# When VectorE's queue reaches its work: conversions and tables moved in the prologue of a graph-attention kernel

## Chip, cores and metric

One core of one Trainium2 chip. The metric is device time in microseconds of one execution. Engines: TensorE (PE in the profile), VectorE (DVE), ScalarE (ACT), GpSimd (POOL) and SyncE (SP), each with its own queue, worked through in order. DMAs are issued from the queues of SP, ACT and POOL.

## What is computed

One layer of a graph network on 12500 nodes of 256 features and 200000 edges sorted by their destination:

```python
h = relu(layernorm(x))                         # x: 12500 x 256
q, k, v = h @ Wq + bq, h @ Wk + bk, h @ Wv + bv     # 8 heads of 32
logits = sum(q[dst] * k[src], over 32) / sqrt(32)   # 200000 edges x 8 heads
attn = softmax of the logits over the edges of one dst
agg = segment_sum(attn * v[src], dst)
o = gelu(agg + h @ Wskip + bskip)
x = x + layernorm(h + o) * gamma + beta
```

## The kernel before

It works in two stages. **The prologue** (`project`, L156, and `make_plan`, L422) makes tables in DRAM. **The walk** (`walk_streams`, L760) goes along the edges, gathers rows of those tables and reduces them. The walk begins when the prologue has ended: its first instructions stand behind a branch (L349) on a flag that the plan computes.

`project` goes over 98 blocks of 128 nodes, in 23 groups of 1, 2, 4, then sixteen times 5, then 4, 4, 2 and 1 blocks (L168). `prepare(g)` (L201) loads the x tile of group g+2 (L180, three buffers), takes mean and variance of each block (L211, L215), their factors (L221, L222), and ACT makes h (L226). For each block PE transposes h (L140) and ACT copies that to SBUF (L142); PE then multiplies it with the weights of keys and values (L257, into ps_kv, three buffers) and of queries (L263, into ps_q, one buffer). VectorE evicts both, adding the bias: L260 for keys and values, L267 for queries. ACT and POOL split q into two parts (L268, L269), and SP stores h, kv and q (L272, L274).

Among this stands other work of VectorE, put there by a scheduler that places each instruction by its own estimate of when its inputs are there; "kept order" dependencies (`behind`, L161) hold an instruction back behind another one of its engine without a semaphore:

- `pieces` (L112, called in group 3): the biases as three bf16 parts.
- `make_near` (L703, called in group 4): the tables of node offsets, near and near_n, 48 partitions wide, in five parts. Each part has two iotas of POOL (L711, tiles near_m and near_g, one buffer each, so the iota of a part waits for L753 of the part before) and some ten operations of VectorE (L740 to L753). Its first operation (L716) is kept behind the factors of the latest group. The walk reads these tables (L1052, L1063).
- `make_plan`: loads the destinations (L406, L408), checks their order (L443 to L446), writes them and the sources to DRAM (L441, L449), computes where each of 8 streams starts (L459 to L478), and gathers the chunks of all streams, 66 x 8 x 384 destinations and as many sources, with 16 indirect DMAs of POOL (L488). VectorE casts them to float: L507 the destinations (df), L492 the sources (sf). From df come the first node of each step (L512 to L517, stored and read back by L518, L519 as one row, d0_row), what L523 to L608 make of that row, the masks and offsets of L636 to L683 that go to e_tab and pen_tab, and at last the flag (L700). sf is transposed by PE (L496, kept behind the products of blocks from the middle on) and cast into idx (L504), by which the walk gathers.

The lines that set the gathers and casts:

```python
488   nc.gpsimd.indirect_dma_start(out=t[:, s, :CH], ..., ap=at_i[:, s:s + 1]...)
492   nc.vector.tensor_copy(sf[:, :, :CH], sch)
507   nc.vector.tensor_copy(df[:, :, :CH], dch[:, :, :CH])
```

Of the kernel before, what the change touches and what calls it, by code (L numbers as in the profile page):

```python
# [34 lines left out]
OP = mybir.AluOpType  # L35
# [12 lines left out]
S = 8  # L48
K = 3
CH = K * P  # L50
# [20 lines left out]
def gnn_kernel(ctx: ExitStack, tc: tile.TileContext, x, src, dst, Wq, bq, Wk, bk, Wv, bv,  # L71
               Wskip, bskip, gamma, beta, out):
    nc = tc.nc
    N, HID = x.shape
# [4 lines left out]
    KV = 2 * HID  # L79
# [25 lines left out]
    def weights(t, w):  # L105
        return nc.sync.dma_start(t, w.rearrange("(c p) n -> p c n", p=P))

    def rows(t, a):
        return nc.scalar.dma_start(t, bass.AP(tensor=a.tensor, offset=a.offset,
                                              ap=[[0, t.shape[0]], [1, HID]]))  # L110
# [26 lines left out]
    def transposed(pool, psum, h):  # L137
        ps = psum.tile([P, KC, P], F32, name="ps_t")
        for c in range(KC):
            nc.tensor.transpose(ps[:, c, :], h[:, c * P:(c + 1) * P], ident)  # L140
        hT = pool.tile([P, KC, P], F32, name="hT")
        return hT, nc.scalar.copy(hT, ps)  # L142
# [13 lines left out]
    def project():  # L156


        last, turned, products = None, None, []

        def behind(ins, other):  # L161
            tc.add_manual_dep(ins.ins, other.ins.name, mybir.DependencyInfo(
                mybir.DependencyClass.NoSync, mybir.DependencyReason.DATA), reason="kept order")

        sizes = [1] * NBLK
        if NBLK >= 14:
            mid = NBLK - 14
            sizes = [1, 2, 4] + [5] * (mid // 5) + [mid % 5] * (mid % 5 > 0) + [4, 2, 1]  # L168
        with tc.tile_pool(name="proj_c", bufs=1) as cpool, \
# [21 lines left out]
            b_q = cpool.tile([P, HID], F32, name="b_q")  # L191
# [41 lines left out]
            for g, (b0, n) in enumerate(zip(starts, sizes)):  # L233

                if g > 1 and g + 1 < len(sizes):
                    ready[g + 1] = prepare(g + 1)
                if g == 4:
                    make_near(tc, near, near_n, lambda ins: behind(ins, last))
                if g == 3:
                    for ins in [rows(gam, gamma)] + \  # L240
                            [weights(w_s, Wskip)]:
                        behind(ins, products[-1])
                    pieces(b_s3, bskip, 1.0)
                    pieces(b_o3, beta, 1.0)
                    zero = cpool.tile([WN, HID], F32, name="zero")
                    nc.vector.memset(zero, 0.0)
                    for k in range(2):
                        behind(nc.scalar.dma_start(q_pc[NP:, k * HID:(k + 1) * HID], zero),
                               products[-1])
                h = ready.pop(g)  # L250
                kvo = pool.tile([P, 5, KV], F32, name="kvo")[:, :n, :]
                qp = pool.tile([P, 5, 2, HID], F32R, name="qp")[:, :n]
                for b in range(n):
                    hT, turned = transposed(pool, psum, h[:, b, :])
                    ps_kv = psum.tile([P, 2 * HID], F32, name="ps_kv", bufs=3)
                    for c in range(KC):
                        ins = nc.tensor.matmul(ps_kv, hT[:, c, :], w_kv[:, c, :], start=c == 0,  # L257
                                               stop=c == KC - 1)
                    products.append(ins)
                    nc.vector.tensor_tensor(kvo[:, b, :], ps_kv, b_kv, op=OP.add)  # L260
                    ps_q = psum.tile([P, HID], F32, name="ps_q", bufs=1)
                    for c in range(KC):
                        ins = nc.tensor.matmul(ps_q, hT[:, c, :], w_q[:, c, :], start=c == 0,  # L263
                                               stop=c == KC - 1)
                    products.append(ins)
                    q = qp[:, b, 1, :].bitcast(F32)
                    nc.vector.tensor_tensor(q, ps_q, b_q, op=OP.add)  # L267
                    nc.scalar.copy(qp[:, b, 0, :], q)  # L268
                    nc.gpsimd.tensor_tensor(qp[:, b, 1, :], q, qp[:, b, 0, :].bitcast(F32),  # L269
                                            op=OP.subtract)  # L270
                for tab, t in ((h_tab, h), (kv_tab, kvo)):
                    nc.sync.dma_start(tab[b0 * P:(b0 + n) * P, :]  # L272
                                      .rearrange("(p b) d -> p b d", p=P), t)
                nc.sync.dma_start(q_pc[b0 * P:(b0 + n) * P, :]  # L274
                                  .rearrange("(p b) d -> p (b d)", p=P),
                                  qp.rearrange("p b k d -> p (b k d)").bitcast(F32))
                if g < 2:
                    ready[g + 1] = prepare(g + 1)
        return products

    def queries(q_tab):

# [41 lines left out]
    NST = -(-(LEN + LEN // 128) // (CH - 1))  # L324
# [10 lines left out]
    idx = pl.tile([P, S, K, NST], I32, name="idx")  # L335
    d0_row = pl.tile([1, NST * S], I32, name="d0_row")
    slot_row = pl.tile([1, NSLOT // 2, 4], I32, name="slot_row")
    near = pl.tile([6 * S, QT * P], BF16, name="near")
    near_n = pl.tile([6 * S, 4 * WNN + 4 * WN], BF16, name="near_n")
    e_tab = dram.tile([NST, 6 * S, CH], BF16, name="e_tab")  # L340
    pen_tab = dram.tile([NST, 2, S, CH + 1], F32, name="pen_tab")
    with tc.tile_pool(name="pln", bufs=1) as pool, tc.tile_pool(name="pln_e", bufs=1) as ep, \
            tc.tile_pool(name="pln_ps", bufs=1, space=PSUM) as psum:
        products = project()
        make_plan(tc, pool, ep, psum, src, dst, N, LEN, NST, SLACK, NT, dram, ident, flag,
                  idx, d0_row, slot_row, e_tab, pen_tab, products, 4 * HID, 4 * KV)
    fits = nc.values_load(flag[0:1, 0:1], min_val=0, max_val=1)
    many = nc.values_load(flag[0:1, 2:3], min_val=0, max_val=1)
    with tc.If(fits > 0) as branch:  # L349
# [47 lines left out]

def load_edges(nc, pool, a, E, C, fill, name):

    t = pool.tile([P, C], I32, name=name)  # L400
    full, rest = divmod(E, C)
    nc.vector.memset(t, fill)

    for lo, hi in ((0, full // 16 * 16), (full // 16 * 16, full)):
        if lo < hi:
            nc.gpsimd.dma_start(t[lo:hi], a[lo * C:hi * C].rearrange("(p c) -> p c", c=C))  # L406
    if rest:
        nc.gpsimd.dma_start(t[full:full + 1, :rest], a[full * C:].rearrange("(p c) -> p c", p=1))  # L408
    return t


def load_next(nc, pool, dst, E, C, N):

    nxt = pool.tile([P, 1], I32, name="nxt_i")
    nc.vector.memset(nxt, N)
    starts = E // C if E % C else E // C - 1
    nc.gpsimd.dma_start(nxt[:starts], bass.AP(tensor=dst.tensor, offset=dst.offset + C,
                                              ap=[[C, starts], [1, 1]]))
    return nxt


def make_plan(tc, pool, ep, psum, src, dst, N, LEN, NST, SLACK, NT, dram, ident, flag, idx, d0_row,  # L422
              slot_row, e_tab, pen_tab, products, bytes_x, bytes_row):

    nc = tc.nc
    E = src.shape[0]
    STEP = CH - 1
    C = -(-max(E, (S - 1) * LEN + SLACK + STEP * NST + 1) // P)  # L430
    dst_p = dram.tile([1 + P * C, 1], I32, name="dst_p")
    src_p = dram.tile([1 + P * C, 1], I32, name="src_p")
    d0_d = dram.tile([NST, S], I32, name="d0_d")
# [26 lines left out]
    last = pool.tile([NST, S], F32, name="last")  # L460
# [23 lines left out]
    dch = pool.tile([NST, S, CH + 1], I32, name="dch")  # L484
    sch = pool.tile([NST, S, CH], I32, name="sch", tag="sch")
# [3 lines left out]
                out=t[:, s, :CH], out_offset=None, in_=tab[:, :],  # L489
                in_offset=bass.IndirectOffsetOnAxis(ap=at_i[:, s:s + 1], axis=0))  # L490
    sf = pool.tile([NST, S, CH + 1], F32, name="sf")
    nc.vector.tensor_copy(sf[:, :, :CH], sch)  # L492
    for s in range(S):
        ps = psum.tile([P, K, NST], F32, name="ps_i")
        for j in range(K):
            ins = nc.tensor.transpose(ps[:, j, :], sf[:, s, j * P:(j + 1) * P],  # L496
                                      ident[:NST, :NST])
# [6 lines left out]
        nc.vector.tensor_copy(idx[:, s], ps)  # L504

    df = pool.tile([NST, S, CH + 1], F32, name="df")
    nc.vector.tensor_copy(df[:, :, :CH], dch[:, :, :CH])  # L507

    nc.vector.tensor_copy(df[0:1, 1:, 0:1], df[0:1, 1:, 1:2])
    nc.vector.memset(df[0:1, 0:1, 0:1], 0.0)  # L510
# [9 lines left out]
                                      ap=[[0, 1], [1, NST * S]]))  # L520

    line = pool.tile([1, 2, S], F32, name="line")
    nc.vector.tensor_copy(line[:, 0, :], d0_row[:, :S])  # L523
    nc.vector.tensor_copy(line[:, 1, :], d0_row[:, (NST - 1) * S:])
    nn = pool.tile([1, S + 1], F32, name="nn")
    nc.vector.memset(nn, float(N))
    nc.vector.tensor_copy(nn[:, :S], line[:, 0, :])
# [11 lines left out]
    F = NST * S  # L539

    done = ep.tile([1, 2, F], F32, name="done2", tag="chk_d")
    done, more_b = done[:, 0], done[:, 1]
# [6 lines left out]
    nc.vector.tensor_scalar(lead_i, lead_i, P - 1, None, op0=OP.bitwise_and)  # L549
    nc.vector.tensor_copy(lead, lead_i)  # L550
    nc.vector.tensor_scalar(lead, lead, -1.0, float(P - 1), op0=OP.mult, op1=OP.add)
    nc.vector.tensor_copy(done[:, :F - S], d0_row[:, S:])
    nc.vector.tensor_tensor(done3[:, :NST - 1], done3[:, :NST - 1],
                            nn[:, None, :S].to_broadcast([1, NST - 1, S]), op=OP.subtract)
    nc.vector.tensor_copy(done3[:, NST - 1], cnt[:, 0])
# [58 lines left out]
    for i, size in enumerate((bytes_x, bytes_row)):  # L614
        nc.vector.tensor_scalar(slot_row[:, :, 2 * i:2 * i + 2],
                                ps[:, i, :M].rearrange("o (m b) -> o m b", b=2), float(size),
                                None, op0=OP.mult)
# [46 lines left out]
    def row(r, make):  # L664
# [5 lines left out]
                                             op=OP.is_equal))  # L670
# [1123 lines left out]
```

## Time and profile before

| | us |
|---|---|
| median of three runs (2444.04 to 2455.95) | 2448.26 |
| the profiled execution, its own time | 2449.12 |
| its span, first to last instruction | 2447.3 |
| prologue: last eviction of block 97 (L267) ends | 355.6 |
| walk: first gather (L1035) starts | 359.1 |

The profiled execution is 0.9 us above the median. Busy shares of the span are PE 70%, DVE 82%, ACT 44% and POOL 68%; as averages over two stages of different kind they say little on the prologue, which has to be read from its own stretch.

How to read the lines shown below. A line of the timeline has the start and the duration in us, the engine, the line of the program, the operation, output and inputs with partitions x elements and type, how many instructions are merged, and in brackets how long the engine sat idle before it and what ended that. A line of the waits has who waited for whom, the total in us, how many times, and the longest. A line of the table of stretches has the stretch, its length, the busy time of each engine with its count of instructions, the granted TensorE clock (1.00 is full speed), the busy share of the 16 DMA engines and what they moved.

### The profile page before, as it was taken

Reading aid. Unit: us, or ns where it says so; the run is one execution under the profiler, and the core shown is the slowest. Engines: PE = TensorE matmul, PEld = TensorE weight load, DVE = VectorE, ACT = ScalarE, POOL = GpSimd, SP = SyncE. Lnnn points to the kernel's source line nnn. Section 1 sums busy time; section 2 is a strip of 40 time slices with the busy share of each in tenths; the row PEclk is TensorE's granted clock in tenths of the full one; section 3 lists DMA queues with packets and bytes.
Section 4 is the critical chain, followed back from the end, with each engine's and each line's share of the span. In section 5 each row is a group of like instructions: output and inputs, shape, how many; then the busy total and the mean of one; then the engine's idle time right before and its main releaser. Section 6 shows DMA issues by size and latency. Waiting matters only on the chain.

```text
span 2447.3 us, 29473 instructions
## 1 busy us (share of the span) xinstructions
PE 1708.7 (70%) x7824; PEld 909.6 (37%) x7824; DVE 1999.8 (82%) x2461; ACT 1066.4 (44%) x2328; POOL 1658.1 (68%) x1745
## 2 busy tenths in 40 slices
PE   6879983555557767767777767676676777677765
PEld 3445542222223333333333334333333343343333
DVE  7866856777778898898888888888888988888884
ACT  3333321333334544554545444445444444445443
POOL 4342447777777777777777777777777777777740
PEclk9999995666667777776667676677677767767678
DMA  7656668888888988888888988899889888889862
GB/s 259 253 207 264 251 250 263 256 255 254 255 268 266 286 276 282 285 277 284 279 285 279 287 271 282 274 285 288 275 282 287 282 281 284 277 279 287 279 202 76
DMA packets 306128, 649.33 MB, mean 265 GB/s; under 512 B 52836, under 2 KB 192238, under 8 KB 300954
## 3 DMA queue, kind: packets, MB, share of 16 engines
q0 software_dynamic: 128768, 423.23, 55.7%
q1 hardware_dynamic: 176434, 223.46, 27.2%
q8 instruction: 64, 1.05, 0.2%
q10 hardware_dynamic: 748, 0.66, 0.1%
q14 instruction: 114, 0.93, 0.1%
HBM read 538.91 MB, written 108.23 MB: 264 GB/s over the span
## 4 chain that ended last, share of the span: by engine, by line
DMA 25%; PE 23%; DVE 19%; issue 12%; POOL 10%; ACT 8%; SPq 3%; DVEq 0%; another core or an unknown queue 0%; ACTq 0%; POOLq 0%
DMA kv<-kv_tab,idx 16%; POOL kv L1035 9%; PE ps_kv L257 5%; DVE kv L1084 5%; DMA h<-h_tab 4%; PE ps_a L867 4%; DVE vw L1139 3%; DVE L L1091 3%; PE ps_qe L1075 3%; PE ps_q L263 3%; PE ps_a L1165 2%; ACT L987 2%; PE ps_hot L909 2%; DMA out_dram<-o 2%; SPq L837 2%
## 5 line engine op out<-in xcount | busy, mean ns | idle before, releaser
L1035 POOL DMA_INDIRECT kv<-kv_tab,idx x1576 | 1521.3, 965 | 482.4 <-issue 342.6
L1084 DVE TENSOR_TENSOR kv<-ps_qe,kv 128x1024 f32<-128x1024 f32 x394 | 468.8, 1218 | 191.1 <-DMA kv<-kv_tab,idx 117.9
L1139 DVE TENSOR_TENSOR vw<-ps_x,kv 128x2048 f32<-128x2048 f32 x197 | 449.4, 2281 | 9.1 <-PE ps_x L1126 9.1
L1091 DVE TENSOR_REDUCE L<-kv 128x64 f32<-128x2048 f32 x197 | 450.4, 2286 | 6.9 <-DMA et<-e_tab 0.2
L1075 PE MATMUL ps_qe<-qw,to_e 64*128 64x256 f32 (+1 forms) x1576 | 312.6, 396 | 107.5 <-DVE kv L1084 102.6
L1054 ACT ACTIVATE to_e<-ps_hot,ones 128x384 fp32r<-128x384 f32 x396 | 210.4, 573 | 316.1 <-PE ps_hot L1052 308.0
L1075 PEld LDWEIGHTS ps_qe<-qw,to_e 64*128 64x128 f32 (+1 forms) x1576 | 223.8, 248 | 272.7 <-DVE kv L1084 168.4
L1165 PE MATMUL ps_a<-vw,to_n 128*32 128x264 f32 (+1 forms) x2344 | 280.3, 516 | 4.2 <-DVE vw L1146 3.7
L1177 ACT COPY sums_w<-ps_a 128x264 f32<-128x264 f32 x130 | 49.2, 378 | 498.3 <-PE ps_a L1165 439.7
L1099 PE MATMUL ps_x<-ident,L 128*64 128x128 f32 x197 | 73.1, 371 | 274.0 <-DVE vw L1146 205.2
L1052 PE MATMUL ps_hot<-et,near 48*128 48x384 bf16 x396 | 142.5, 420 | 136.5 <-ACT to_e L1054 131.8
L257 PE MATMUL ps_kv<-w_kv,hT 128*128 128x512 f32 x392 | 194.8, 619 | 15.3 <-ACT hT L142 14.2
L269 POOL TENSOR_TENSOR qp<-qp 128x256 fp32r<-128x256 f32 x98 | 88.4, 903 | 171.8 <-ACT qp L268 171.6
L867 PE MATMUL ps_a<-w_s,hT 128*128 128x256 f32 x368 | 171.9, 648 | 21.2 <-ACT hT L853 18.0
L1165 PEld LDWEIGHTS ps_a<-vw,to_n 128*32 128x32 f32 (+1 forms) x2344 | 99.3, 139 | 216.2 <-issue 174.4
L1099 PEld LDWEIGHTS ps_x<-ident,L 128*64 128x64 f32 x197 | 25.7, 130 | 362.7 <-DVE vw L1146 288.3
L1165 PE MATMUL ps_hot<-vw,to_n 128*64 128x264 f32 x808 | 144.8, 509 | 1.9 <-DVE o L915 1.1
L1183 ACT COPY kv<-ps_a 1x264 f32<-1x264 f32 x388 | 142.9, 368 | 6.3
L867 PEld LDWEIGHTS ps_a<-w_s,hT 128*128 128x128 f32 x368 | 115.6, 329 | 69.0 <-ACT hT L853 44.1
L987 ACT ACT_TABLE_LOAD x102 | 130.9, 1283 | 1.7
L1065 ACT ACTIVATE to_n<-ps_hot,ones 128x384 f32<-128x384 f32 x197 | 103.6, 578 | 53.7 <-PE ps_hot L1063 51.8
L263 PE MATMUL ps_q<-w_q,hT 128*128 128x256 f32 x392 | 106.1, 395 | 24.3 <-DVE qp L267 24.2
(278 smaller groups left out, 2103.2 us busy)
## 6 DMA issues: line engine op xcount, KB each, us to landing
qw<-q_pc SPq DMA_DIRECT2D x264, 128.0 KB
kv<-kv_tab,idx POOLq DMA_INDIRECT x1576
kv_tab<-kvo SPq DMA_DIRECT2D x16, 1280.0 KB
q_pc<-qp SPq DMA_DIRECT2D x16, 1280.0 KB
qw<-q_pc SPq DMA_DIRECT2D x264, 64.0 KB
table<-sums_w SPq DMA_DIRECT2D x264, 61.9 KB
pen<-pen_tab SPq DMA_DIRECT2D x66, 192.5 KB
sums<-table SPq DMA_DIRECT2D x92, 132.0 KB
```

The costliest lines, as they stand in the source:

```text
L257: ins = nc.tensor.matmul(ps_kv, hT[:, c, :], w_kv[:, c, :], start=c == 0, stop=c == KC - 1)
L263: ins = nc.tensor.matmul(ps_q, hT[:, c, :], w_q[:, c, :], start=c == 0, stop=c == KC - 1)
L867: self.keep(nc.tensor.matmul(self.ps[:, b, :], self.hT[:, b, c, :], w_s[:, c, :], start=False, stop=False, skip_group_check=True))
L987: keep(nc.scalar.activation(dummy[:, 1:2], dummy[:, 0:1], function))
L1035: ins = keep(nc.gpsimd.indirect_dma_start(out=t[:, s, :], out_offset=None, in_=kv_tab[:, :], in_offset=bass.IndirectOffsetOnAxis(ap=idx[:, ...
L1054: keep(nc.scalar.activation(step[c]["to_e"][:, i, :], ps[:, :CH], AF.Relu, scale=-1.0, bias=ones))
L1075: keep(nc.tensor.matmul(ps[:, b, a, :], g["to_e"][at:at + w, i, j * P:(j + 1) * P], g["qw"][at:at + w, i, :], start=True, stop=True))
L1084: keep(nc.vector.tensor_tensor(k, g["qe", half].rearrange("p b a d -> p a b d"), k, op=OP.mult))
L1091: keep(nc.vector.tensor_reduce(g["L"][:, j, :].rearrange("p (s h) -> p s h", s=S), g["kv"][j][:, :, :HID].rearrange("p s (h d) -> p s h d" ...
L1139: keep(nc.vector.tensor_tensor(t[:, :, HEADS:].rearrange("p s (h d) -> p s h d", h=HEADS), wj[:, :, :, None].to_broadcast([P, S, HEADS, D] ...
L1165: keep(nc.tensor.matmul(ps[at:at + w, :], g["to_n"][:, j, i * P + at:i * P + at + w], g["vw"][j][:, s, :], start=j == 0, stop=j == tiles_o ...
L1183: keep(nc.scalar.copy(step[c + 1]["kv"][0][0:1, s, HID - HEADS:], ps[at:at + 1, :]))
```

## The change

`project` now returns its evictions of the queries (L267) in order as well, as `biased`. `make_plan` keeps five casts behind one of them, counted in hundredths of the 98 blocks: the destinations (L507) behind block 35 (36 hundredths), the sources (L492) behind block 42 (43), and three casts of d0_row (L523, L524, L552) behind block 44 (45). With 16 groups or more, `make_near` is called in group 13 (whose first block is 57) where it was called in group 4 (block 12), and `pieces`, with the loads of gamma and Wskip and the two stores of zeros, in group 12 where it was group 3. Nothing is computed differently, and no instruction is added or left out. Lines from 431 on move by seven.

```diff
-                if g == 4:
+                if g == (4 if len(sizes) < 16 else 13):
                     make_near(tc, near, near_n, lambda ins: behind(ins, last))
-                if g == 3:
+                if g == (3 if len(sizes) < 16 else 12):
                     for ins in [rows(gam, gamma)] + \
                             [weights(w_s, Wskip)]:
                         behind(ins, products[-1])
...
-                    nc.vector.tensor_tensor(q, ps_q, b_q, op=OP.add)
+                    biased.append(nc.vector.tensor_tensor(q, ps_q, b_q, op=OP.add))
...
+    def behind(ins, share):
+
+        tc.add_manual_dep(ins.ins, biased[len(biased) * share // 100].ins.name,
+                          mybir.DependencyInfo(mybir.DependencyClass.NoSync,
+                                               mybir.DependencyReason.DATA), reason="kept order")
...
-    nc.vector.tensor_copy(sf[:, :, :CH], sch)
+    behind(nc.vector.tensor_copy(sf[:, :, :CH], sch), 43)
...
-    nc.vector.tensor_copy(df[:, :, :CH], dch[:, :, :CH])
+    behind(nc.vector.tensor_copy(df[:, :, :CH], dch[:, :, :CH]), 36)
...
-    nc.vector.tensor_copy(line[:, 0, :], d0_row[:, :S])
-    nc.vector.tensor_copy(line[:, 1, :], d0_row[:, (NST - 1) * S:])
+    behind(nc.vector.tensor_copy(line[:, 0, :], d0_row[:, :S]), 45)
+    behind(nc.vector.tensor_copy(line[:, 1, :], d0_row[:, (NST - 1) * S:]), 45)
...
-    nc.vector.tensor_copy(done[:, :F - S], d0_row[:, S:])
+    behind(nc.vector.tensor_copy(done[:, :F - S], d0_row[:, S:]), 45)
```

## The prediction

> **What bounds the kernel now.** The chain of work that ended last, taken over the first 600 us, shows two stages. Until 355 us it runs through PE's projection matmuls (L257 19.8% of that stretch, L263 10.8%); after that through the gathers of the walk (POOL L1035, DMA kv) and VectorE's L1084, L1091 and L1139. The change touches the first stage alone, so I read that one: 98 blocks, each with two transposes, a key/value product (L257) and a query product (L263), both evicted by VectorE (L260, L267).
>
> PE's timeline gives its pace and where it loses it. Columns: start, duration, instruction, and in brackets the idle time before it with what ended it.
>
> ```profile
> 78.78 1.60 PE L263 MATMUL ps_q<-w_q,hT 128*128 128x256 f32 x4 [2.64 <-DVE qp L267]
> 80.17 3.15 PE L257 MATMUL ps_kv<-w_kv,hT 128*128 128x512 f32 x4
> ...
> 134.31 2.07 PE L263 MATMUL ps_q<-w_q,hT 128*128 128x256 f32 x4 [4.05 <-DVE qp L267]
> ...
> 154.61 2.07 PE L263 MATMUL ps_q<-w_q,hT 128*128 128x256 f32 x4 [6.56 <-DVE qp L267]
> ...
> 208.72 1.98 PE L257 MATMUL ps_kv<-w_kv,hT 128*128 128x512 f32 x4
> ...
> 214.88 1.98 PE L257 MATMUL ps_kv<-w_kv,hT 128*128 128x512 f32 x4
> ```
>
> From 208.72 to 214.88 PE does two blocks: **3.08 us a block** when nothing holds it. The three upper stalls have one cause: ps_q has a single buffer, so the query product of a block waits until VectorE has evicted that of the block before. I count the starts of L257 block by block: block 0 at 12.58, 7 at 46.99, 17 at 86.64, 28 at 120.14, 41 at 177.22, 57 at 227.20, 97 at 352.23. Against 3.08 a block, the stretch 7-17 is 8.9 us late (39.65 for 30.8), 17-28 on time (33.5 for 33.9), 28-41 **17.0 late** (57.08 for 40.04), 41-57 0.7 and 57-97 1.8 late. The first seven blocks lose 12.9 to loads and first transposes.
>
> Who holds VectorE is in its waits of the first 480 us (total, times, longest) and in its own timeline:
>
> ```profile
> DVE kvo L260 <- PE ps_kv L257: 42.7, 35, 2.3
> ...
> DVE st L211 <- DMA x_in<-in_x_dram: 10.0, 6, 4.3
> ...
> DVE sf L492 <- DMA sch<-src_p,at_i: 7.9, 1, 7.9
> DVE df L507 <- DMA sch<-src_p,at_i: 6.0, 1, 6.0
> DVE near_s L740 <- POOL near_m L711: 5.0, 4, 2.1
> ```
>
> ```profile
> 131.39 1.94 DVE L507 CAST df<-dch 66x3072 f32<-66x3072 int32 x1 [5.96 <-DMA sch<-src_p,at_i]
> ...
> 151.22 1.76 DVE L492 CAST sf<-sch 66x3072 f32<-66x3072 int32 x1 [7.94 <-DMA sch<-src_p,at_i]
> ```
>
> The first line of the waits is harmless: VectorE waiting for PE means PE is the bound. The casts L507 and L492 are the fault: VectorE's queue is in order, each stands in it before its gathered chunk has landed, and the evictions behind it wait too. PE's 4.05 and 6.56 us of idle follow from them.
>
> The table of stretches says the same in busy time (PE, PEld, DVE, ACT, POOL, then granted clock, DMA share, GB/s):
>
> ```profile
> 47.00:87.00 40.00, 32.84 (x101) 17.83 (x102) 33.79 (x107) 11.58 (x31) 15.26 (x21) 0.96 0.48 177
> 87.00:120.00 33.00, 31.51 (x108) 18.46 (x107) 26.67 (x83) 15.47 (x40) 13.82 (x19) 1.00 0.95 335
> 120.00:177.00 57.00, 42.37 (x134) 24.23 (x132) 39.29 (x108) 14.96 (x39) 26.88 (x30) 0.91 0.58 218
> 177.00:258.00 81.00, 78.31 (x287) 47.40 (x287) 48.14 (x139) 33.85 (x89) 22.05 (x28) 1.00 0.70 257
> ```
>
> In 177-258 VectorE is busy 48 of 81 us and PE 78: there is room for VectorE's work. In 47-87 it is busy 33.8 of 40, beside waits: the near tables stand there.
>
> **The change part by part.** How VectorE's queue stands in the built program, counted in evicted blocks (L260) ahead of an instruction, before and after: sorted check (L445) 19 and 9; offsets for the gathers (L478) 25 and 15; L507 29 and 37; the big subtraction L640 31 and 39; L492 33 and 52; the node-row conversions L523 and L552 35 and 53; L573 40 and 60; the near tables 6 to 15, and, but for part 0's first six operations, 41 to 51. L492 is pinned only behind block 42; the scheduler puts it after the near tables. The last of the plan (L700) stands at 89 and 90.
>
> *The two waits.* The gathers issue from 113.97 to 142.14 on POOL, the first chunk has landed by 131.39 and the second by 151.22: 17 and 37 us after the first issue. After the change they start some ten blocks earlier, at block 15, and the casts stand 22 and 37 blocks later (68 and 114 us at 3.08). Both waits go, and with them the whole loss of 28-41: two stalls, the slowed matmuls behind each (2.07 for 1.03) and the 4.27 us wait for an x tile before, which gathers, x loads and the src store shared the queues with. **-17.0**. If only the two waits go and the x wait stays, it is 1.8 less (PE's idle of 1.82 at 123.83).
>
> *The node row.* Its way from L517 (135.4) to L523 (156.38) took 21 us, POOL's gathers in between; after, 39 to 53 is 14 blocks, 43 us. 0. L573 to L589 (way through DRAM) had 8.0 us (175.9 to 183.9), with 0.74 of wait left; after it has again three blocks, 9.2 us. Between 0 and +1; I take 0. The transposes of sf (L496) stand on PE behind block 52's products, L492 on VectorE ahead of that block's eviction; as ps_q keeps PE close behind VectorE, I take 0, at most +1.8 (L492's own time).
>
> *The near tables, gone from 6-15.* Their groups sum to 25.9 us of durations (four parts of 256 columns 19.5, the one of 128 4.2, small ones 2.2); starts lie some 0.07 closer than durations over 72 operations, so 21, and 5.0 of waits for POOL's iota. In their place the plan's first checks move up: L402 1.0, L445 2.0, L446 1.7, L459 0.7, L463 1.2, L466 1.2 and small ones 1.6, 9.4, with 1.7 of part 0. A block's own work on VectorE is 1.40 (L260 0.61, L267 0.34, L211 0.34, L215 and the factors 0.11, start to start), so each block leaves 1.68: over blocks 7-17 16.8, more than 11.1. PE should keep pace: up to **-8.9**. Against it stand the x loads. Groups now come due sooner in a stretch where DMA share was 0.80 (12-47); landings took 5.3 and 6.5 us (issue 101.97, 114.94; use 107.30, 121.45), with three buffers. Cost from 0 to the whole 8.9; I give +3, two waits of the size that cost PE 1.82 less a little overlap. Net **-5.9**.
>
> *The near tables, now in 41-51.* About 19 us of work fall on ten blocks with 16.8 free, then L492 1.7 and the first idx casts. Each part's L740 waits for an iota that starts only when L753 of the part before is done (1.5 us, behind which one or two evictions fit): four waits that were 5.0 in all. Below: VectorE's backlog is worked off in 52-63 without PE stopping, 0. Above: 2.2 + 1.7 + 5.0 = 8.9. As ps_q is single, I go near the middle, **+4.5**. 57-97 is the same work in the same order but for the k chain (some 5 us later on blocks that had room): 0, bounds -1 and +3. POOL moves the iotas of four parts (near_m of 1.5 or 1.2 us each, near_g 0.4); its subtractions have 2 to 4 us of idle each, so only the store of q lags. The loads of gamma, W_s and the zero rows (0.4 MB) go to block 52 or so on ACT's and SP's queues: at 257 GB/s there, 0.
>
> Here the TensorE clock is weighed. After 2.64 us of idle the next eight matmuls took 1.60 + 3.15 instead of 1.03 + 1.88: 1.84 lost. The Trainium skill (TensorE: Matmul & The Clock Gate, What's actually happening) puts the fall to half clock at an idle window of about 3.4 us. By it, stalls of 1 to 2 us in the middle cost no clock, and the sum stays; by the row one long one might add 1.8.
>
> **The sum:** -17.0 - 5.9 + 4.5 = -18.4. The walk starts when block 97 is done (its first gather comes 4 us after), and keeps its length. The profiled execution, 2449.1 us (span 2447.3 and 1.8 around it), lies 0.9 over the median of three (2448.3). 2449.1 - 18.4 = 2430.7; against the median 2429.9. I say **2430**.
>
> **Rivals.** *The x loads take the early gain* (0.14): 87-120 ran at 0.95 of DMA, and the same bytes now come sooner. Nothing in 7-17, two or three landings waited for later at 1.82 each: -17.0 + 4.5 + 4.5 = -8, 2441; range 2437 to 2444. Against: 47-87 used 0.48. *VectorE becomes the bound in 41-57* (0.11): 8.9 with one cold clock 1.8, and 2 more in 57-63: -17.0 - 5.9 + 12.7 = -10, 2439, range 2436 to 2446. *All of it pays* (0.08): early stretch on pace, middle nearly free: -17.0 - 8.9 + 1 = -25, 2424 and down to 2418. *Slower* (0.06): one mechanism, x tiles late at VectorE's L211. If six groups between blocks 7 and 41 each wait a whole landing of 6.5 us, that is 39 against 25.9 given up, with 4.5 in the middle: +17.6, 2467. It decides from four groups on (21.4 / 6.5 = 3.3). *The pins move nothing* is ruled out by the queue order. The forecast keeps 0.61, 2424 to 2437.
>
> Range 2420 to 2442: it leaves out the slow ends of the first two rivals, the slower case and the lowest of the best one, some 0.2. About 0.5%, 12 us, is what a measurement of this kernel can tell from no change, so faster means under 2436: the forecast but for its upper edge and the best case, 0.68; same 0.26, slower 0.06.
>
> **What the next profile would show.** No wait of L492 or L507 (now L499, L514) for DMA; no idle of PE over 3 us behind L267 after block 7; L257 of block 41 near 154 instead of 177; iota waits of about 1 us each now between 155 and 185 us with short PE stalls behind L267 there; the first walk gather near 340 instead of 359. Wrong if: x_in waits over 10 us in the first 120; PE falling behind more than 9 us in 41-57; or a walk longer than 2088 us (359 to the end) by more than 3.

## The result

| | before | after |
|---|---|---|
| median (6 runs each) | 2448.48 (2444.04 to 2455.95) | 2432.33 (2431.09 to 2434.58) |
| ratio, 95% interval | | 0.9935 (0.9922 to 0.9948) |
| profiled execution, own time | 2449.12 | 2432.86 |
| last eviction (L267) of block 97 starts | 355.2 | 334.8 |
| first gather of the walk | 359.1 | 339.1 |
| first gather to the end of the span | 2088.2 | 2092.0 |

The kernel is 16.1 us faster, 0.65%; the forecast was 2430. The prologue gained 20.05 us where 18.4 were forecast, and the walk of the profiled pair gave 3.8 back. In the first eight experiments the walk alone took 2633 to 2713 us, so their totals are compared only with runs of the kernel before made beside them; their prologues kept the same pace.

PE's timeline of after (columns as before) has four stalls of more than 0.3 us behind L267 left after block 7, and none over 2.70 us:

```profile
161.55 1.13 PE L263 MATMUL ps_q<-w_q,hT 128*128 128x256 f32 x4 [0.55 <-DVE qp L267]
...
175.43 1.13 PE L263 MATMUL ps_q<-w_q,hT 128*128 128x256 f32 x4 [0.86 <-DVE qp L267]
...
179.77 1.13 PE L263 MATMUL ps_q<-w_q,hT 128*128 128x256 f32 x4 [0.49 <-DVE qp L267]
...
185.32 1.13 PE L263 MATMUL ps_q<-w_q,hT 128*128 128x256 f32 x4 [2.70 <-DVE qp L267]
```

All four lie where the tables now stand. Seen from the block that waits, each is VectorE being late; the records before them show why. VectorE's waits of the first 480 us in after:

```profile
DVE kvo L260 <- PE ps_kv L257: 44.2, 29, 2.3
...
DVE st L211 <- DMA x_in<-in_x_dram: 11.1, 9, 3.6
```

No cast waits for a DMA any more (13.9 us before), and the x tiles cost VectorE 1.1 more than before. The rise lies ahead of block 7: between 48 and 180 us the waits for x tiles fell from 6.2 to 3.8 us, the longest from 4.3 to 1.2. The stretches of after (PE, PEld, DVE, ACT, POOL, clock, DMA share, GB/s):

```profile
47.00:87.00 40.00, 37.96 (x130) 22.03 (x129) 32.36 (x103) 14.63 (x39) 25.66 (x30) 1.00 0.91 343
87.00:120.00 33.00, 31.21 (x110) 18.35 (x109) 16.90 (x46) 13.26 (x36) 12.92 (x17) 1.00 0.72 258
120.00:177.00 57.00, 53.06 (x180) 30.49 (x178) 42.34 (x120) 22.25 (x57) 22.80 (x29) 1.00 0.72 263
177.00:258.00 81.00, 75.19 (x269) 43.78 (x270) 74.99 (x206) 31.27 (x80) 30.04 (x31) 1.00 0.65 248
```

In 47-87 PE is busy 37.96 of 40 us instead of 32.84, in 120-177 53.06 instead of 42.37. In 177-258 it lost 3 us of busy time, and VectorE rose from 48 to 75 us of 81.

For all kernels below I read one thing: the starts of VectorE's eviction of the queries (L267, 98 records in every profile). "Late" is the time of a stretch less 3.08 us a block. The order within a pair of blocks shifts a start by up to 1.5 us, so only differences of one column count.

| kernel | block 7 at | late 7-17 | 17-41 | 41-57 | 57-97 | block 97 at | first gather | ratio to before, 95% |
|---|---|---|---|---|---|---|---|---|
| before | 52.0 | 7.0 | 16.5 | 1.5 | 1.1 | 355.2 | 359.1 | |
| after | 48.7 | 0.5 | -0.8 | 7.5 | 1.6 | 334.8 | 339.1 | 0.9935 (0.9922-0.9948) |
| after_again | 48.8 | 0.9 | -0.9 | 7.8 | 1.6 | 335.4 | 339.6 | 0.9948 (0.9932-0.9965) |
| pins_only | 51.8 | 5.5 | 2.0 | 1.5 | 1.3 | 339.2 | 343.1 | 0.9986 (0.9964-1.0008) |
| tables_only | 48.9 | 2.8 | 11.8 | 7.8 | 1.5 | 349.9 | 353.9 | 0.9991 (0.9971-1.0011) |
| near8 | 48.3 | 1.7 | 10.2 | 1.5 | 1.5 | 340.5 | 344.5 | 0.9928 (0.9905-0.9951) |
| near9 | 46.7 | 3.1 | 10.2 | 2.6 | 1.0 | 340.8 | 344.8 | 0.9935 (0.9915-0.9956) |
| near17 | 49.4 | 0.5 | -0.7 | 1.5 | 7.8 | 335.7 | 339.6 | 0.9964 (0.9945-0.9983) |
| spread7_p3 | 50.7 | 3.0 | 5.3 | 1.6 | 1.3 | 339.1 | 343.1 | 0.9957 (0.9940-0.9973) |
| spread13_p3 | 50.5 | 4.7 | -0.8 | 4.9 | 3.7 | 340.2 | 344.4 | 0.9956 (0.9939-0.9972) |
| thin | 49.8 | 3.3 | 0.0 | 8.0 | -0.4 | 337.9 | 342.1 | 0.9928 (0.9915-0.9942) |
| thick | 50.2 | 1.7 | 5.4 | 1.6 | 1.6 | 337.7 | 341.6 | 0.9928 (0.9915-0.9942) |
| no_tables | 48.9 | 1.9 | -0.9 | 1.8 | 1.4 | 330.3 | 334.2 | 0.9910 (0.9897-0.9924) |
| thin_k | 47.4 | 2.3 | -0.1 | 2.8 | 0.2 | 329.9 | 334.1 | 0.9925 (0.9911-0.9939) |

Each row is one profile. The two of the changed kernel agree within 0.6 us at every column but the ratio, but thin and thin_k, whose programs are alike in these blocks, are 2.4 us apart at block 7, so single rows scatter by that much there. The ratios scatter more: a few us of the prologue are hardly seen in them.

### The profile page after: what moved, and what is told of

Its sections match the earlier page's. It is cut to its first block, busy times and chain, and to the rows that moved or that the text cites. A ratio compares the mean times of both kernels' runs of the same rounds, so it can differ in the third digit from the quotient of the medians.

```text
span 2431.1 us, 29470 instructions
## 1 busy us (share of the span) xinstructions
PE 1704.8 (70%) x7824; PEld 904.9 (37%) x7824; DVE 2000.1 (82%) x2461; ACT 1067.8 (44%) x2328; POOL 1671.5 (69%) x1745
## 4 chain that ended last, share of the span: by engine, by line
DMA 26%; PE 21%; DVE 17%; POOL 13%; issue 13%; ACT 6%; SPq 2%; POOLq 0%; DVEq 0%; another core or an unknown queue 0%; ACTq 0%
DMA kv<-kv_tab,idx 19%; POOL kv L1042 13%; PE ps_kv L257 5%; DVE kv L1091 4%; DVE vw L1146 4%; DVE L L1098 4%; DMA h<-h_tab 3%; PE ps_a L874 3%; PE ps_q L263 3%; PE ps_qe L1082 2%; PE ps_a L1172 2%; ACT L994 1%; SPq L844 1%; DMA out_dram<-o 1%; PE ps_hot L1059 1%
## 5 line engine op out<-in xcount | busy, mean ns | idle before, releaser
L257 PE MATMUL ps_kv<-w_kv,hT 128*128 128x512 f32 x392 | 193.7, 615 | 16.1 <-ACT hT L142 15.3
L269 POOL TENSOR_TENSOR qp<-qp 128x256 fp32r<-128x256 f32 x98 | 97.4, 994 | 155.2 <-ACT qp L268 154.9
```

## The experiments

**The two halves.** pins_only keeps the pins and calls tables and pieces in groups 4 and 3; tables_only has the tables late and no pins. In pins_only

```diff
-                if g == (4 if len(sizes) < 16 else 13):
+                if g == (4 if len(sizes) < 16 else 4):
-                if g == (3 if len(sizes) < 16 else 12):
+                if g == (3 if len(sizes) < 16 else 3):
```

and in tables_only, for this and the other four casts,

```diff
-    behind(nc.vector.tensor_copy(sf[:, :, :CH], sch), 43)
+    nc.vector.tensor_copy(sf[:, :, :CH], sch)
```

> The five pins kept, tables and bias pieces called in groups 4 and 3 again. By the built order the gathers then stand behind block 25 (15 in the changed kernel), L514 behind 37 and L499 behind 43, the tables between blocks 6 and 15. Theory (PE loses what VectorE waits, and what VectorE cannot do in the 1.68 us that each block leaves it): both cast waits gone, blocks 28 to 41 gain their 17, blocks 7 to 17 keep their loss of 8.9, blocks 41 to 57 lose about 1 instead of 7.9. 2448.5 - 17 = 2431.5, and up to 1.8 more for an x wait: 2431 to 2434, level with the changed kernel at 2432.3; the move of the tables is then worth nothing. Rival (the pins work only because the gathers start earlier): gathers from about 114 still crowd the x loads, half the 17 comes back, 2440.

> Tables and bias pieces called in groups 13 and 12, no pin. By the built order the gathers stand behind block 15, L514 behind 19 and L499 behind 23, so the casts follow their gathers as closely as before. In the changed kernel the first gather went out at 70.0 us; with 17 and 37 us to land, as before, L514 (block 19, near 85) waits about 2 and L499 (block 23, near 98) about 9. Theory: the waits are back at a smaller size, about 9 to 12 us of PE's time with the cold matmuls, and blocks 41 to 57 lose some 6; 2438 to 2447, likeliest 2442. Rival (the earlier gathers alone remove the waits, the pins do nothing): 2432, with no wait of L499 or L514 above 1 us.

The pins alone take 17-41 from 16.5 to 2.0 late and the first gather from 359.1 to 343.1, 16.0 of the 20.05. The tables' move alone brings 5.2, and beside the pins 4.0 (343.1 against 339.1), where I had expected nothing. So the rival on pins_only (half the gain) falls in the prologue. Its total does not show the gain: 16.0 of 3051 us would be a ratio of 0.9948, and the interval, 0.9964 to 1.0008, leaves that out and holds 1. What offset the gain in its walk is not known; no profile of before was taken beside it. In tables_only both waits are back, although the gathers start ten blocks earlier; VectorE's timeline:

```profile
89.27 1.76 DVE L514 CAST df<-dch 66x3072 f32<-66x3072 int32 x1 [4.71 <-DMA sch<-src_p,at_i]
...
106.09 1.76 DVE L499 CAST sf<-sch 66x3072 f32<-66x3072 int32 x1 [5.47 <-DMA d_d<-d_i]
```

(The second is named for another transfer that landed last by the profile; a cast of sch waits for its chunk.) Earlier gathers only brought the casts forward with them: 10.2 us of waits, and blocks 17 to 41 are 12.5 later than in after. It is the pin that removes a wait.

**Where the tables stand.** near8, near9 and near17 are the changed kernel with `make_near` called in group 8, 9 or 17; after_again is the changed kernel itself.

> As the changed kernel, tables called in group 8 instead of 13. By the built order they stand between blocks 17 and 27, gathers behind block 13, casts behind 37 and 43. In the changed kernel VectorE was busy 26 of 54 us between 76 and 130 us, and 30.7 of 32 between 166 and 198. Theory (the place's free time of VectorE decides): blocks 41 to 57 lose 1 instead of 7.9, blocks 17 to 28 lose up to 1; 2432.3 - 6 = 2426, range 2423 to 2429, faster than both kernels. Rival (the tables cost PE the same wherever they stand, through their waits for the iotas and through sharing with POOL): the 7 are lost in 17 to 28 instead, 2432.

> Tables unspread, called in group 9: by the built order at blocks 22 to 31, behind the last gather on POOL instead of among the gathers, and where VectorE was most idle. Theory (the chain of a part is the price, not the place): 5 to 6 lost between blocks 22 and 35 where near17 lost 0.9, last L267 at 335. Rival (the place's free time decides, and near8 was slow only for the iota behind the gathers): 1 lost, last L267 at 330.

> As the changed kernel, tables called in group 17. By the built order they stand between blocks 62 and 72, and the last of the plan (L707) behind block 95 instead of 90. In the changed kernel VectorE was busy 46 of 48 us between 246 and 294. Theory (the place's free time decides): blocks 41 to 57 gain back 7, but the 21 to 25 us of tables meet the masks, of which VectorE can take perhaps half in the 24 us it had free after block 57: 10 to 12 lost, 2436, range 2431 to 2443. Rival (the loss in 41 to 57 is the meeting of tables with cast L499 and the node row, not a lack of free time): anywhere else they are free, 2426.

> The changed kernel once more, for its walk on this chip (the walk took some 600 us more in the four runs before this than in the first profiles) and for the scatter. Its last L267 should end its wait at 334.8 again, first gather 339.1, since the prologues of the first four kernels ran at the same 3.08 us a block. Two views of the walk: its length is scatter (then the first gather tells the change's worth and totals scatter by 10 us), or it depends on the program (then this kernel's total stands with near8 at 3032 and not with near17 at 3040 or pins_only at 3048).

My theory, that a place where VectorE is idle takes the tables for nothing, fell. Wherever they went, 41-57 came down to 1.5 to 2.6, and the loss went with them: 11 us in 17-41 (near8, near9), 6.2 in 57-97 (near17), where I had expected 10 to 12 in a full stretch and, for near8, 1 in an empty one. In near8 part of the loss is a queue that I had not looked at: the second part's iota stands behind the gathers on POOL.

```profile
88.58 0.94 POOL L495 DMA_INDIRECT sch<-src_p,at_i  x1 [0.18 <-issue]
89.55 1.55 POOL L718 IOTA near_m<- 48x256 f32 x1
```

```profile
91.13 0.42 DVE L747 TENSOR_TENSOR near_s<-near_m 48x256 f32<-48x256 f32 x1 [4.66 <-POOL near_m L718]
```

The matmuls behind two of near8's three longer stalls also ran slow, 2.07 us instead of 1.13. near9 has its iotas behind all gathers and lost as much, more than either of its expectations (5 to 6, or 1). There the bias pieces follow at blocks 33 to 38; near8 has them at 29 to 34 and loses nothing in 28 to 41, so the pieces alone are not the rest of near9's 11 us. Its VectorE also waits 3.06 us at 142.76 for the load of beta (L121), and PE's stall of 1.31 us at 145.43 comes behind that; the remainder stays open.

**Is it the chain of iotas?** The five parts kept in groups of their own, so that each iota is long done. `make_near` becomes a generator that yields after each part; the pieces are in group 3. In spread7_p3

```diff
-                if g == (4 if len(sizes) < 16 else 13):
-                    make_near(tc, near, near_n, lambda ins: behind(ins, last))
+                if g == (4 if len(sizes) < 16 else 7): tables = make_near(tc, near, near_n, lambda ins: behind(ins, last))
+                if g >= (4 if len(sizes) < 16 else 7): next(tables, None)
...
-            nc.vector.tensor_mul(sq, n, n)
+            late(nc.vector.tensor_mul(sq, n, n))
```

and in spread13_p3 the same with 13 for 7.

> The tables' five parts each kept behind a group of its own from group 7 on (by the built order at blocks 13, 17, 22, 27, 32), bias pieces in group 3, pins kept. So far the tables cost PE 5 to 6 us in blocks 7 to 17, 41 to 52 and 62 to 72 alike, and 11 at 17 to 27, where a part's iota stood behind POOL's gathers. Theory now: the price is the chain of a part, its iota on POOL, its table on VectorE, the next iota, in which VectorE stands, and its operations that run slow beside the iota. With five blocks between the parts each iota is done before VectorE needs it: no wait of near_s for near_m, the tables cost 0 to 1.5; last eviction of block 97 (L267) at 329 to 331 instead of 334.8, first gather near 334. Rival (some 20 us of VectorE's work must push PE back, since ps_q has one buffer): 335 and 339.

> As the last one, but the parts from group 13 on (blocks 42, 46, 52, 57, 62), beside cast L499 (block 45) and the node row. Theory (the chain of a part is the price): 0 to 2 instead of the 5.9 that the tables took between blocks 41 and 57, last L267 at 329 to 331. Rival (VectorE's work itself): 335; and if the meeting with the node row counts, between the two, 332 to 333.

The second theory fell too: both kernels end their evictions later (339.1 and 340.2) than theory and rival said. In spread7_p3 the waits for near_m are gone, but three for near_g took 3.7 us, so it decides little. In spread13_p3 the waits for iotas are nearly gone between 130 and 240 us,

```profile
DVE near_g L759 <- POOL near_g L718: 1.0, 2, 0.8
```

yet 41-57 and 57-97 together are 5.4 later than in no_tables (4.9 + 3.7 against 1.8 + 1.4). Its blocks 7 to 17 are 4.7 late instead of 0.5, but not by the tables. With the pieces in group 3 the plan's two checks (L452, L453) stand in one block, 1.78 and 1.77 us on either side of its L267, where after has them one block apart; PE did not stop there. It stopped at 61.67 (0.79 us) and 66.65 (2.13), after VectorE had stood for an x tile and, behind that, had two conversions of the plan (L466, L470: 1.51 and 1.24 us) in one block:

```profile
59.94 0.43 DVE L211 BATCH_NORM_STATS2 st<-x_in 128x6 f32<-128x256 f32 x1 [3.01 <-DMA x_in<-in_x_dram]
```

```profile
61.67 1.13 PE L263 MATMUL ps_q<-w_q,hT 128*128 128x256 f32 x4 [0.79 <-DVE qp L267]
...
66.65 1.13 PE L263 MATMUL ps_q<-w_q,hT 128*128 128x256 f32 x4 [2.13 <-DVE qp L267]
```

**How much stands between two evictions.** The generator yields after two to six operations, and `late` keeps each chunk behind the newest L267: one chunk a block from block 17 on (thin), two from block 23 on (thick, which has 23 and a second `next`); the pieces are in group 5. The tables' operations add up to 28.2 us of durations in thin, 27.3 in thick and 28.5 in after (sums over the traces), so the work is nearly the same.

```diff
                     biased.append(nc.vector.tensor_tensor(q, ps_q, b_q, op=OP.add))
+                    if len(biased) > 17:
+                        next(tables, None)
```

In no_tables the tables are left out:

```diff
-                    make_near(tc, near, near_n, lambda ins: behind(ins, last))
+                    nc.gpsimd.memset(near, 0.0)
+                    nc.gpsimd.memset(near_n, 0.0)
```

> Each of the tables' five parts cut into four chunks of two to six operations, one chunk kept behind the query eviction of each block from block 17 on (by the built order blocks 18 to 37); bias pieces in group 5, which leaves the plan's first checks one to a block as in the changed kernel; pins kept. So far the tables, in pieces of five or more us to two blocks, cost PE 5 to 8 us in every place tried, and spreading whole parts did not help. Theory now (a block leaves VectorE 1.68 us; what stands between two evictions beyond that stops PE at once through the one ps_q, and PE, always at its own pace, never makes it up): chunks of 0.8 to 1.5 us cost nothing. Blocks 17 to 28 late by -1.4 and 41 to 57 by 1.6, as where no tables stand; last L267 at 329 to 331 instead of 335.1, first gather near 334; in all some 5 us less than the changed kernel. Rival (20 us of further VectorE work push PE back in any form): 335.

> The same chunks, but two behind each eviction from block 23 on (by the built order blocks 24 to 34), when POOL has issued the gathers. Theory (what counts is the work between two evictions): 2 to 3 us a block over ten blocks against 1.68 free, and L515 to L648 come after it: 5 to 8 lost, last L267 at 334 to 337. Rival (the chain of a part with its iotas is the price, the density is not): the chain is no longer than in the thin form, so the same 329 to 331 as there.

> The changed kernel without the tables: make_near is not called, and POOL sets the two tables to zero, so the offsets that the walk reads are zero. It shows all that the tables cost the prologue where they stand now. By the late blocks of 41 to 57 (7.5 to 7.8 with tables, 1.5 without) 6 us: last L267 at 329, first gather at 333. If the tables are hidden after all and the loss in 41 to 57 belongs to cast L499 and the node row, 334 to 335. The walk does the same work on other numbers; should its length change by more than the scatter of 10, the totals say nothing on the tables.

Without tables 41-57 is 1.8 late instead of 7.5, so they cost PE 5.8 in the changed kernel, and the cast and node row next to them nothing that shows. One chunk a block costs 0.9 in 17-41 (0.0 against -0.9), two cost 6.3 (5.4), with 2.9 us of waits for iotas among them.

So nearly the same work costs little or much by how long VectorE is away between two evictions. What makes it long is not fully taken apart: thick also has an operation that stood 1.95 us beside an iota (L769), and thin has neither that nor, but for 0.3 us, the waits. spread13_p3 has 1.0 us of waits and one such operation, 1.96 us (L764 at 217.51), before its longest stall (2.31 at 222.79). Its other stalls, up to 0.86 us, are what dense work cost with hardly a wait.

But thin as a whole won nothing: the row that goes through DRAM, which the prediction had at 0 to 1 and the expectation at nothing, was now read too early.

```profile
203.12 0.15 DVE L597 TENSOR_SCALAR k<-wide 128x1 f32<-128x1 f32 x1 [7.04 <-DMA wide<-gvu_d]
```

From the start of L581 (188.82), which makes the row, to here are 14.3 us, and 52-57 is 7.5 late. The same fault as that of the two casts, in a third place.

**The third wait.** thin_k is thin with one pin more.

```diff
-    nc.vector.tensor_scalar(k[:, 1:2], wide[:, 0, F - 1:], -1.0, None, op0=OP.add)
+    behind(nc.vector.tensor_scalar(k[:, 1:2], wide[:, 0, F - 1:], -1.0, None, op0=OP.add), 59)
```

> The kernel of thin, with one pin more: the first reader of the row that comes back through DRAM (L597, k from wide) is kept behind block 57 (by the built order it stands at 58 instead of 54). In thin the tables cost 0.9 in blocks 17 to 41, but L597 waited 7.0 us for wide, and blocks 52 to 57 were 7.5 late instead of 1.2. From L581 (block 51, 188.8 us) to the landing of wide took 14.2 us, 4.6 blocks; the new place is 7 blocks behind. Theory (every such wait stops PE, and only for what VectorE's queue holds at its head): blocks 52 to 57 late by about 1.2, nothing late after it, last L267 at 331.5 instead of 337.9, first gather near 335.8; total 6 less than thin, 2426 beside a kernel before of 2448, ratio 0.990 to 0.991. Rival (the row's work moved behind block 57 meets the masks, which fill VectorE from 66 to 90): half of it lost again there, last L267 at 334 to 335, 2429.

The wait is gone, 41-57 falls from 8.0 to 2.8 and nothing is late after it. The last L267 is at 329.9, level with no_tables. From block 7 on thin_k is 5.3 late in all, no_tables 4.2 and after 8.9: the tables are hidden but for some 1 us. Of the 8 us between thin and thin_k 2.4 lie before block 7 and 1.0 in 7-17, where the two are alike, and are chance. The rival (half the loss comes back behind block 57) fell, but the total expected, 2426, was met only by the profiled run. The median, 2429.84, is 2.2 below thin's and 2.5 below that of the changed kernel, and the intervals overlap; the profiled run, 2425.68, is the lowest of its five (the highest is 2433.32). It beats the kernel before by 0.75%; that it beats the changed one is likely, not shown.

## Why the prediction was right, and where its terms were off

- **The two casts, -17.0.** Blocks 17 to 41 went from 16.5 to -0.8 late: -17.2. Mechanism and size held: pins_only, with the tables where they were, gives 14.5 of it, and tables_only keeps both waits.
- **Blocks 7 to 17, -5.9.** 7.0 to 0.5, so -6.4, and 3.3 more before block 7, which I had not counted: -9.7 in all; of the 3.3 some is chance (thin and thin_k differ by 2.4 there). The +3 for x tiles was wrong: behind block 7 the x_in waits fell, and in 47-87 the queues took 0.91 of DMA without stopping PE. The rival that x loads eat the gain, and the slower case, had no such wait.
- **The tables in 41 to 51, +4.5.** 1.5 to 7.5, +6.1: short by 1.6, the term that was mis-sized. The place was right, the account only in part. It set 19 us against the 16.8 that ten blocks leave; but spread13_p3 has the same work on some twenty blocks and lost 5.4, and thin has it on twenty and lost 0.9. So a sum over blocks does not give the loss; what counts is how long VectorE is away between two evictions. Of the 5.0 us of iota waits only 1.7 came; in their place one operation ran slow beside an iota, 1.69 us instead of 0.29 in before. The 2.70 us stall at 185.32 comes behind this, here on VectorE and on POOL:

```profile
182.22 0.67 DVE L260 TENSOR_TENSOR kvo<-ps_kv,b_kv 128x512 f32<-128x512 f32 x1
182.82 1.69 DVE L764 TENSOR_SCALAR near_n<-near_g,near_e 48x4 bf16<-48x4 f32 x1
184.51 0.42 DVE L747 TENSOR_TENSOR near_s<-near_m 48x256 f32<-48x256 f32 x1
184.86 0.41 DVE L267 TENSOR_TENSOR qp<-ps_q,b_q 128x256 f32<-128x256 f32 x1
```

```profile
182.37 2.11 POOL L718 IOTA near_m<- 48x256 f32 x1 [1.41 <-DVE near_n L760]
```

  The same operation on 48x4 took 0.22 us at 191.37, with no iota beside it. The Trainium skill (SBUF — State Buffer, Who interferes with whom) says that VectorE and GpSimd share a port pair under an exclusive lock. These lines agree: the iota began first, and L764 ended at 184.51, 0.03 us after the iota (182.37 + 2.11 = 184.48). The iota itself was not slowed: this one, of the fifth part, took 2.11 us in every kernel that has it, in before and thin too, where no operation was held up beside it.
- **57 to 97, the node row, the k chain: 0.** +0.5, a wait of 0.3 at k. Right, but with less room than I thought: in thin the same read waited 7.0 us.
- **The walk, unchanged.** 3.8 longer in the pair of profiles, so one of the three signs of being wrong, a walk longer than 2088 us by more than 3, came true. Its gathers are POOL's, one after the other, here in before and in after (count, then least, median and longest ns):

```profile
L1035 POOL DMA_INDIRECT kv<-kv_tab,idx x1576: 949/953/1781, 359.1 to 2359.6; - x197
```

```profile
L1042 POOL DMA_INDIRECT kv<-kv_tab,idx x1576: 952/957/1847, 339.1 to 2345.3; - x197
```

  Some 4 ns a gather over 1576 are 6 us. thin, thick, no_tables and thin_k had walks of 2090.7, 2089.1, 2087.6 and 2089.7, so walks scatter by 3 us, and the 2092.0 of after lies 1.3 above the longest of them. The interval of the ratio, 12.7 to 19.1 us of gain, also leaves out the 20.05 of the prologue. Whether the change lengthens the walk by a few us stays open.
- **The clock.** I weighed a stall of 2.64 us that had cost 1.84, and expected one long stall of the middle perhaps to cost as much. The one of 2.70 cost nothing (1.13 behind it, granted clock 1.00). In pins_only the matmuls behind the very stall of before, again 2.64 us, ran at a granted clock of 1.00, where before has 0.68 and then 0.61:

```profile
78.57 1.13 PE L263 MATMUL ps_q<-w_q,hT 128*128 128x256 f32 x4 [2.64 <-DVE qp L267]
79.54 1.88 PE L257 MATMUL ps_kv<-w_kv,hT 128*128 128x512 f32 x4
```

  while in near8 the granted clock was 0.50 behind a stall of 2.42 us:

```profile
115.89 2.07 PE L263 MATMUL ps_q<-w_q,hT 128*128 128x256 f32 x4 [2.42 <-DVE qp L267]
```

  The Trainium skill (TensorE: Matmul & The Clock Gate, What's actually happening) has the window of about 3.4 us running freely, not started by the kernel. That a stall of 2.4 to 2.7 us may or may not cost the clock fits such a window. The stall of 2.42 us does not fit 3.4 us as the least that costs it; here the measurement decides.

Of the sum, -18.4, the prologue gave -20.05: the stretches up to block 41 were 4.0 better, the middle 1.6 and the rest 0.5 worse, and the first gather came 0.3 later behind the last L267. By the starts of L257, which the prediction counted, blocks 7 to 17 gained the whole 8.8 and 41 to 57 lost 7.3, so two errors of nearly 3 us, x tiles and tables, cancelled. With the walk's 3.8 against the surplus of the prologue, that the total came within 2.4 us of the forecast is in part luck.

## What to carry to other kernels

Here PE set the pace with a single output buffer for the queries, and time that it lost was never made up. Ask of the engine that frees such a buffer not how busy it is, but how long it is away between two of its evictions, waits included. Spread over twenty blocks, some 1.4 us a block (28.2 / 20, an estimate from the durations), the tables cost 0.9 us; over ten to twelve blocks, some 2.5 a block, they cost some 5 to 6 us, and 11 in near8 and near9, where other waits came on top. No run gave ps_q a second buffer, so that the single one makes the evictions urgent is read from PE's waits behind L267 and was not tried. And when a queue is packed differently, look at each reader of a DMA again: an instruction that hardly waited (0.7 us in before at L589, 0.3 in after at L596) may stand far ahead of its data in the next order.

## What the runs showed beside that

The same kernel's walk took 2092 us in one profile and 2638 in another (after_again), with the same prologue to 0.6 us. Medians of the kernel before on chip 1 were 3051 us beside the first runs and 2449 beside the last, so it is not a matter of the chip alone. In the longer walk gathers took as long (957 ns at the median), but engines stood together again and again, here PE for 5.99 us and VectorE for 6.39, which VectorE's timeline puts down to no engine or DMA of this core:

```profile
999.23 2.36 DVE L1091 TENSOR_TENSOR kv<-ps_qe,kv 128x1024 f32<-128x1024 f32 x2 [6.39 <-remote]
```

What held them stays open. It adds scatter to totals (near8 has a lower ratio than near17 with a first gather 4.9 later), and is why the verdicts here rest on the prologue's records.
